# Seven products for eight in one more product of gate and up (S3 T3), with new orders of the stages

## The chip, the cores and the metric

The kernel runs on one core of one Trainium2 chip. The metric is the device time in microseconds (us), taken as the median of several runs.

## What is computed

Two layers in float32 on x of shape (2, 2048, 512). The first is an attention over the embedding axis: q, k, v are products of the normalized x with 512 x 512 weights, the scores are a 512 x 512 matrix for each of the two batches. The second is a gated network whose weights are looked up in a table of 16 values:

```
x = x + attention(layernorm(x))            # scores = q^T k / 4, softmax, times v, times Wo
n = layernorm(x)
gate = n @ lut[gate_idx].T                 # 1376 features
up   = n @ lut[up_idx].T
out  = x + (silu(gate) * up) @ lut[down_idx].T
```

The change lies in the two products with 1376 features, gate and up, which take 461 of 1063 us.

## The kernel before, in words

**Stages in time.** Gram matrices of the normalized x (to 80 us), 512 x 512 products for the scores and weights (to 174), the attention's output y (to 286), gate and up (286 to 747), the last 96 features by rows (747 to 789), the down product (to the end).

**Gate and up.** The 1376 features are 10 blocks of 128 (index f) and a rest of 96; the 4096 tokens are 8 chunks of 512, taken in 4 pairs (index p). A unit is one block and one pair (class `GateUp`, L1071). Gate and up of a block, and the two chunks of a pair, form a 2 x 2 scheme of blocks, whose 8 block products are made with 7 (Strassen's scheme in Winograd's form): "11"x"11" (stage a1), "S2"x"T2" (a2), "S1"x"T1" (a3), "S4"x"22" (a4), "S3"x"T3" (c1), "22"x"T4" (c2), "12"x"21" (b). Each is two matmuls of 128 x 128 by 512 columns, since a half of the 512 inputs is two blocks of 128. The results add up in PSUM (2 KB banks of 128 x 512) and, copied by ACT or added by DVE, in SBUF: p1, p7 (what c1 gives), u2, c22, h0, h1 and y. A hidden chunk h0 or h1 goes to DRAM (`hd`) by SP's queue.

**Second level.** From f = 2 on, four units form a group: two blocks (f even, f + 1) and two pairs (p even, p + 1). Within a group three of the seven products are themselves made with 7 matmuls for 8, by class `Second` (L948): `of_b` for "12"x"21", `of_c` for "22"x"T4", `of_d` for "S4"x"22", in the PSUM banks x, z and w. A unit's place in its group is its role: 0 (f even, p even), 1 (f even, p odd), 2 (f odd, p even), 3 (f odd, p odd). Roles 0 and 1 of a group follow each other; so do 2 and 3, but they come a whole row of units later (order of units: f, then p). So partial sums that roles 0 and 1 make for roles 2 and 3 are kept in DRAM: `part` (L1010) copies a bank with ACT and stores it as r6 or r5. Role 1 stores both for each `Second` on ACT's queue. Role 2 adds a further product onto r5 by an accumulating DMA from POOL (`onto=True`). They come back through `add_part` (L1023), an accumulating DMA from DRAM onto p1 or u2, or through `back` (L1028), a plain load into y, both from POOL: r6 in role 2, r5 in role 3. The second level's sums of tokens (T1, T2, T4 of each `Second` and group) are made once, kept in DRAM (`far`), and loaded by ACT's queue before each use (`loads`, L1049): for role 1 T1 and T2, for role 2 T4. Their buffers are rings: RT = 3 for parts, TT = 8 for these loads (L1034). p1, p7, c22, y and h1 have one buffer each, u2 and h0 two.

**Order.** PE, ACT, DVE and SP keep the order in which the program writes their instructions; POOL's is set by the framework's scheduler. `Line.run` (L1239) writes the stages of a unit, with those of the unit before mixed in: a4, first, end and out of the last unit stand within the present one. `between` (L1376) is called between stages: it issues a waiting T load, runs a waiting side job, and then fills DVE with lookups of later weights as long as a planned DVE clock is less than `leads[0]` us ahead of a planned PE clock. Lookups (`copy_predicated`, L342, and `tensor_scalar`, L330) are DVE's largest work.

**Banks.** PSUM has 8: a and c twice, b, x, z and w once (L945). The down product uses a, b and c as well.

**Last rows.** `LastRows` (L1294) computes the 96 last features with the tokens on the rows; every second pair needs sums and negatives of the weights (`weights`), written as side jobs.

Of the kernel before, what the change touches and what calls it, by code (L numbers as in the profile page):

```python
# [69 lines left out]
def tile_attn_ffn(  # L70
# [874 lines left out]
    def psum(tag, name):  # L945
        return fps.tile([P, E], F32, tag=tag, name=name, bufs=2 if tag in "ac" else 1)

    class Second:  # L948
# [8 lines left out]
        def sums(self, g):  # L957
# [4 lines left out]
            def made(tag, u, v):  # L962
                r[tag] = x2p.tile([P, CH], F32, tag="tt", name=f"{tag}_{self.name}{g}", bufs=TT)
                sub(r[tag], u(), v())
                far = self.far[g, tag] = dram.tile(
                    [P, CH], F32, tag=f"{self.name}{g}{tag}", name=f"far_{self.name}{g}{tag}"
                )
                nc.gpsimd.dma_start(far, r[tag])
# [12 lines left out]
        def ready(self, f):  # L981
            return f in gu if self is of_d else f in uw
# [45 lines left out]
        def back(self, u):  # L1028

            t = u.temp("y")  # L1030
            nc.gpsimd.dma_start(t, self.parts[u.p // 2, {2: "r6", 3: "r5"}[u.role]])
            return t

    RT, TT = 3, 8  # L1034
# [7 lines left out]
    seconds = [of_c, of_b, of_d]  # L1042
# [6 lines left out]
    def loads(f, p):  # L1049

        g = p // 2
        if 1 < f < NFT - 1 and f % 2 == 0 and p % 2:
            order = [(of_c, "T2"), (of_c, "T1")]
            order += [(o, tag) for tag in ("T2", "T1") for o in (of_d, of_b)]
        elif 1 < f < NFT - 1 and f % 2 and p % 2 == 0:
            order = [(o, "T4") for o in seconds]
        else:
            order = []
        return [lambda o=o, tag=tag: o.load(g, tag) for o, tag in order]
# [11 lines left out]
    class GateUp:  # L1071
# [32 lines left out]
        def extra0(self):  # L1104
            if self.role == 1:
                of_c.go_on(self, "S2", "T2")
                of_c.part(self, "r6")
            elif self.role == 2:
                of_c.begin(self, "S3", "T3")
                of_c.part(self, "r5", onto=True)  # L1110

        def c1(self):
            self.c = self.view("c")
            mm(self.c, self.pairs("S3", "T3"), True)
            self.p7 = self.temp("p7")
            evict(self.p7, self.c)
# [7 lines left out]
        def c2(self):  # L1124
            if self.role is None:
                mm(self.c, self.pairs("22", "T4"), False)
                add(self.u2, self.c, self.u2)
            elif self.role == 0:
# [3 lines left out]
                add(self.u2, self.c, self.u2)  # L1132
            elif self.role == 1:
                add(self.u2, self.c, self.u2)
                of_c.go_on(self, "S4", "22")
                add(self.u2, of_c.ps, self.u2)
            elif self.role == 2:
                of_c.go_on(self, "22", "T4")

        def extra1(self):  # L1140
            if self.role == 1:
                of_c.go_on(self, "S1", "T1")
                of_c.part(self, "r5")
            elif self.role == 2:
                of_b.begin(self, "S3", "T3")
                of_b.part(self, "r5", onto=True)

        def extra2(self):
            if self.role == 1:
                of_d.go_on(self, "S2", "T2")  # L1150
                of_d.part(self, "r6")
                of_b.go_on(self, "S2", "T2")
                of_b.part(self, "r6")

        def extra3(self):
            if self.role == 1:
                of_d.go_on(self, "S1", "T1")
                of_d.part(self, "r5")
                of_b.go_on(self, "S1", "T1")
                of_b.part(self, "r5")  # L1160
            elif self.role == 2:
                of_d.begin(self, "S3", "T3")
                of_d.part(self, "r5", onto=True)
            if self.role in (2, 3):
                self.y = of_d.back(self)

        def b(self):
# [14 lines left out]
            if self.role != 1:  # L1182
                nc.scalar.activation(h0, self.p1 if self.role in (None, 3) else h0, AF.Silu)

        def silu(self):

            if self.role == 1:
                nc.scalar.activation(self.h0, self.h0, AF.Silu)

        def a3(self):  # L1190
            mm(self.a, self.pairs("S1", "T1"), False)
            self.c22 = self.temp("c22")
            add(self.c22, self.a, self.p7)

        def first(self):
            if self.role == 2:
                add(self.u2, of_c.ps, self.u2)
            if self.role in (2, 3):
                add(self.u2, self.c, self.u2)
            tensor(self.h0, self.h0, self.u2, ALU.mult)  # L1200
            self.store(self.h0, 2 * self.p)

        def kept(self):
            add(self.y, of_d.ps, self.y)
# [28 lines left out]
    class Line:  # L1233
# [5 lines left out]
        def run(self, u, final=False):  # L1239
            last, self.last = self.last, u  # L1240

            role = getattr(u, "role", None)
            u.a1()
            if last is not None:
                last.silu()
            self.between()
            before = getattr(last, "role", None)
            if before == 1:
                last.first()
            u.extra0()  # L1250
            u.c1()
            self.between()
            if before == 2:
                last.kept()
            elif before == 3:
                last.first()
            u.extra1()
            if role != 3 and last is not None:
                last.a4()
                self.between()  # L1260
            u.a2()
            if role == 3:
                self.between(0.0)
                last.a4()
                last.first()
                self.between(0.0)
            else:
                self.between()
            u.extra2()
            u.c2()  # L1270
            if last is not None:
                last.end()
            self.between()
            u.extra3()
            if last is not None:
                last.out()
            one, two = (u.a3, u.b) if final or role in (1, 3) else (u.b, u.a3)
            one()
            self.between()
# [3 lines left out]
            self.between()  # L1283
# [10 lines left out]
    class LastRows:  # L1294
# [17 lines left out]
        def weights(self):  # L1312
            w, v = self.w, self.v
            self.u = u = last_pool.tile([P, KB, 2 * LAST], F32, tag="last", name="last_2")
# [7 lines left out]
                lambda: minus(u[:, 3, :], v[:, 0, :], -1.0),  # L1322
            ]

        def pairs(self, c):

            w, v, u, x = self.w, self.v, self.u, xs[c // 2]
            second = c // 2 % 2
            if c % 2 == 0:
                one, two = (("11", w[:, 0:2, :]), ("21", w[:, 2:4, :], u[:, 0, :], u[:, 1, :]))  # L1330
            else:
                one, two = (("T3", v[:, 2:4, :]), ("22", v[:, 0:2, :], u[:, 2, :], u[:, 3, :]))
            t = x[one[0]]
            out = [(t[:, kk, :], one[1][:, kk, :]) for kk in range(2)]
            t = x[two[0]]
            if second:
                return out + [(t[:, 1, :], two[2]), (t[:, 0, :], two[3])]
            return out + [(t[:, kk, :], two[1][:, kk, :]) for kk in range(2)]
# [35 lines left out]
    leads = [1.4]  # L1374
# [102 lines left out]
    class Down:  # L1477
# [36 lines left out]
        def view(self, tag):  # L1514
            return psum(tag, f"{tag}_d_{self.name}")[:, :H]
# [61 lines left out]
        extra0 = extra1 = extra2 = extra3 = silu = end = out = first  # L1577
# [34 lines left out]
    for (f, p), following in zip(units, units[1:] + [(NFT, 0)]):  # L1612
# [11 lines left out]
        to_load[:] = loads(*following)  # L1624
# [30 lines left out]
    todo += by_two(last_rows.weights() + down_sums(0, hps["dT"]))  # L1655
    n = 0
    for c in (0, 4, 2, 6, 1, 5, 3, 7):
        for half in range(2):
            ps = last_rows.products(c, half, n)
            if n == 0:  # L1660
                line.flush()
            last_rows.rows(c, half, ps)
# [103 lines left out]
```

## Time and profile before

| | us |
|---|---|
| runs | 1064.05, 1063.87, 1063.44 |
| median | 1063.87 |
| profiled execution, its time | 1064.37 |
| its span, first to last instruction | 1062.6 |
| busy: DVE, ACT, POOL | 803.3, 385.1, 108.6 |
| gate and up: start, end | 286.3, 747.1 |

The profile is one execution. Busy time is that of instructions; DMA issues and waits of an engine do not count as busy. A float32 matmul appears as two records, so 128 matmuls are x256. A DMA's share is the part of a stretch in which the 16 DMA engines worked on packets, as a mean over the 16; q0 is POOL's queue, q1 SP's, q10 ACT's. "us to landing" runs from the start of the issuing instruction to the event that says that the data is there. Granted clock was 1.00 throughout.

### The profile page before, as it was taken

Reading aid. Unit: us, or ns where it says so; the run is one execution under the profiler, and the core shown is the slowest. Engines: PE = TensorE matmul, PEld = TensorE weight load, DVE = VectorE, ACT = ScalarE, POOL = GpSimd, SP = SyncE. Lnnn points to the kernel's source line nnn. Section 1 sums busy time; section 2 is a strip of 40 time slices with the busy share of each in tenths; the row PEclk is TensorE's granted clock in tenths of the full one; section 3 lists DMA queues with packets and bytes.
Section 4 is the critical chain, followed back from the end, with each engine's and each line's share of the span. In section 5 each row is a group of like instructions: output and inputs, shape, how many; then the busy total and the mean of one; then the engine's idle time right before and its main releaser. Section 6 shows DMA issues by size and latency. Waiting matters only on the chain.

```text
span 1062.6 us, 11343 instructions
## 1 busy us (share of the span) xinstructions
PE 1055.5 (99%) x3554; PEld 661.3 (62%) x3554; DVE 803.3 (76%) x1538; ACT 385.1 (36%) x725; POOL 108.6 (10%) x160
## 2 busy tenths in 40 slices
PE   8999999999999999999999999999999999999998
PEld 5668887444444444444444444444998888888887
DVE  7888788898998897887988868849756455656554
ACT  4652532455542224444443444444222222211111
POOL 0000000012120120230141023014000000000000
PEclk9999999999999999999999999999999999999999
DMA  8650314589571366696697679569747665666773
GB/s 342 224 186 21 74 25 119 137 225 250 153 217 41 133 232 197 166 201 209 198 188 215 199 170 222 190 205 195 238 149 244 204 211 187 194 195 203 226 227 117
DMA packets 129084, 194.69 MB, mean 183 GB/s; under 512 B 18992, under 2 KB 59184, under 8 KB 127872
## 3 DMA queue, kind: packets, MB, share of 16 engines
q1 hardware_dynamic: 75904, 105.81, 31.4%
q0 software_dynamic: 15776, 39.92, 17.9%
q10 hardware_dynamic: 37344, 48.24, 14.0%
q8 instruction: 28, 0.46, 0.2%
q14 instruction: 32, 0.26, 0.1%
HBM read 111.42 MB, written 82.51 MB: 183 GB/s over the span
## 4 chain that ended last, share of the span: by engine, by line
PE 97%; DVE 1%; ACT 1%; DMA 0%; issue 0%; SPq 0%; ACTq 0%
PE a_g L1065 22%; PE a_d L1065 14%; PE y L839 10%; PE c_g L1065 8%; PE c_d L1065 7%; PE gp L522 6%; PE rows L1349 4%; PE b_d L1065 4%; PE x_g L1065 4%; PE z_g L1065 4%; PE w_g L1065 3%; PE b_g L1065 2%; PE ea_t L675 1%; PE ea_p L675 1%; PE ea_m L675 1%; PE ea_s L675 1%
## 5 line engine op out<-in xcount | busy, mean ns | idle before, releaser
L839 PE MATMUL y<-m,nT 128*128 128x512 f32 x256 | 110.2, 592 | 0.0
L342 DVE COPY_PREDICATED w<-b_w,w 128x1024 f32<-128x1024 int16 (+1 forms) x77 | 98.6, 1280 | 1.4
L839 PEld LDWEIGHTS y<-m,nT 128*128 128x128 f32 x256 | 48.5, 190 | 60.5 <-issue 57.3
L1065 PE MATMUL a_g<-xT_a,s 128*128 128x512 f32 x160 | 75.5, 594 | 0.0
L1065 PE MATMUL a_g<-xb,w 128*128 128x512 f32 x160 | 75.3, 593 | 0.0
L1065 PE MATMUL c_g<-xb,w 128*128 128x512 f32 x160 | 75.2, 592 | 0.0
L1065 PE MATMUL a_d<-dT,hs_a 128*128 128x256 f32 x288 | 72.6, 379 | 0.0
L522 PE MATMUL gp<-xn_a 128*128 128x128 f32 (+3 forms) x256 | 69.9, 434 | 1.7 <-DVE xn_a L223 1.7
L330 DVE TENSOR_SCALAR w<-idx_w,lut_x,lut_sb 128x1024 int32<-128x1024 int32 (+1 forms) x88 | 67.7, 794 | 0.2
L522 PEld LDWEIGHTS gp<-xn_a 128*128 128x128 f32 x256 | 43.9, 190 | 28.4 <-issue 15.1
L172 DVE TENSOR_TENSOR r<-r,p_d 128x256 f32<-128x256 f32 x64 | 27.1, 424 | 44.4 <-ACT p_d L181 41.5
L1065 PEld LDWEIGHTS a_d<-dT,hs_a 128*128 128x128 f32 x288 | 54.5, 189 | 7.7
L1065 PE MATMUL a_g<-xT_sq,s 128*128 128x512 f32 x120 | 56.7, 595 | 0.0
L181 ACT COPY p_d<-a_d 128x256 f32<-128x256 f32 x32 | 11.9, 372 | 121.4 <-PE a_d L1065 121.4
L1065 PEld LDWEIGHTS a_g<-xT_a,s 128*128 128x128 f32 x160 | 30.1, 190 | 38.9 <-issue 36.4
L1065 PEld LDWEIGHTS a_g<-xb,w 128*128 128x128 f32 x160 | 30.3, 190 | 38.5 <-issue 35.9
L1065 PEld LDWEIGHTS c_g<-xb,w 128*128 128x128 f32 x160 | 30.4, 190 | 38.3 <-issue 37.3
L342 DVE COPY_PREDICATED wd<-b_wd,wd 128x1024 f32<-128x1024 int16 (+1 forms) x42 | 50.7, 1208 | 0.8
L172 DVE TENSOR_TENSOR r<-r,a_d 128x256 f32<-128x256 f32 x64 | 26.8, 419 | 29.5 <-PE a_d L1065 29.5
L181 ACT COPY u<-a_g 128x512 f32<-128x512 f32 x40 | 23.4, 586 | 59.9 <-PE a_g L1065 57.3
L172 DVE TENSOR_TENSOR c<-a_g,p 128x512 f32<-128x512 f32 x40 | 27.6, 691 | 20.4 <-PE a_g L1065 19.0
L1349 PEld LDWEIGHTS rows<-last,xb 128*128 128x128 f32 x256 | 41.7, 190 | 0.5 <-issue 0.5
(357 smaller groups left out, 2086.2 us busy)
## 6 DMA issues: line engine op xcount, KB each, us to landing
hd<-h SPq DMA_DIRECT2D x80, 256.0 KB, 3.3
h<-hd SPq DMA_DIRECT2D x40, 512.0 KB, 6.3
nl<-nd SPq DMA_DIRECT2D x32, 256.0 KB, 5.8
xnd<-xn_f ACTq DMA_DIRECT2D x16, 512.0 KB, 4.6
fl<-xnd POOLq DMA_DIRECT2D x32, 256.0 KB, 6.1
xn_back<-xnd SPq DMA_DIRECT2D x32, 256.0 KB, 4.0
rd<-r SPq DMA_DIRECT2D x32, 256.0 KB, 3.2
r<-rd SPq DMA_DIRECT2D x32, 256.0 KB, 4.5
```

The costliest lines, as they stand in the source:

```text
L172: nc.vector.tensor_tensor(dest, a, b, op)
L181: nc.scalar.copy(dest, a)
L330: vec.tensor_scalar(dest.bitcast(I32), idx, lut_x[:rows, k : k + 1], lut_i[:rows, at : at + 1], ALU.bitwise_and, ALU.bitwise_xor,)
L342: vec.copy_predicated(dest, masks[level - 1], t)
L522: nc.tensor.matmul(gp[b][i][:, i * P :], xn[:, i, j % 2, :], xn[:, i:, j % 2, :], start=c % CPB == 0 and j == 0, stop=c % CPB == CPB - 1 a ...
L675: nc.tensor.matmul(ps[:, m, :], self.a[a][:, k, m * P : (m + 1) * P], self.b[b][:, k, :], start=first and m == k == 0, stop=k == 1, skip_g ...
L839: nc.tensor.matmul(ys[k], nTs[k][:, i, :], m[:, i, :], start=(i == 0), stop=(i == KB - 1))
L1065: nc.tensor.matmul(ps, lhsT, rhs, start=first and i == 0, stop=i == len(pairs) - 1, skip_group_check=not first,)
L1349: nc.tensor.matmul(ps[:, jj, :], x[:, j * P : (j + 1) * P], w, start=i == 0, stop=i == len(pairs) - 1,)
```

## The change

A fourth `Second`, `of_e`, makes the product "S3"x"T3" of the four units of a group with 7 matmuls of 128 features for 8, in a PSUM bank e; c then has one bank. What changes by role (in matmuls and in transfers of 256 KB):

- role 0: c1's two matmuls become one that begins e (copied by ACT to bank c) and one onto c.
- role 1: c1's two become three on e (S2 T2, S1 T1, S4 22); two parts more are copied by ACT and stored by its queue; four more T loads for each group and even block go to the ring, of which one is issued late, within role 1.
- role 2: c1's two become two on e (S3 T3, 22 T4); p7 is loaded from r6 of e by POOL, and a part more is added onto r5 by POOL. p7 is then added to u2 by DVE.
- role 3: c1's two go; p7 is loaded from r5 of e by POOL, and r5 of e is also added onto u2 by POOL, after r5 of c.

In the built program, of matmuls with 512 columns there are 691 for 699; ACT has 16 more copies and 40 more DMA issues, POOL 38 more DMA issues, DVE 8 more sums of 512 columns, 16 of 128 and one of 192. The first matmuls of blocks 4, 5 and 6 stand 61 and 45 matmuls apart before, 63 and 41 after.

POOL's order in block 5, by the built program (onto: a part added onto DRAM; r: role): p7 (r2), p1 (r2), onto c, onto e, onto b, u2 (r2), two idx loads, onto d; p7 (r3), p1 (r3), u2 from c (r3), y (r3), u2 from e (r3); p7, p1, onto c, y, onto e, onto b, u2, onto d (r2); p7, p1, u2 from c, y, u2 from e (r3). The y of the first role 2 comes earlier, in block 4.

The core of the diff:

```diff
-        return fps.tile([P, E], F32, tag=tag, name=name, bufs=2 if tag in "ac" else 1)
+        return fps.tile([P, E], F32, tag=tag, name=name, bufs=2 if tag == "a" else 1)
...
-                r[tag] = x2p.tile([P, CH], F32, tag="tt", name=f"{tag}_{self.name}{g}", bufs=TT)
+                r[tag] = x2p.tile([P, CH], F32, tag="rt", name=f"{tag}_{self.name}{g}", bufs=RT)
...
-    RT, TT = 3, 8
+    RT, TT = 3, 7
...
-    seconds = [of_c, of_b, of_d]
+    of_e = Second("e", "e", lambda f: in_two(gu[f]["S3"]), lambda p: in_two(xs[p]["T3"]))
+    seconds = [of_c, of_b, of_d, of_e]
...
+        def c0(self):
+            of_e.begin(self, "11", "11")
+            self.c = self.view("c")
+            evict(self.c, of_e.ps)
+
+        def kept(self, o, a, b, tag, onto=False):
+            (o.begin if onto else o.go_on)(self, a, b)
+            o.part(self, tag, onto)
...
+        def e4(self):
+            of_e.go_on(self, "S4", "22")
+            self.p7 = self.temp("p7")
+            evict(self.p7, of_e.ps)
+            add(self.u2, of_e.ps, self.u2)
+
+        def e3(self):
+            of_e.go_on(self, "22", "T4")
+            add(self.p7, of_e.ps, self.p7)
...
         def a3(self):
             mm(self.a, self.pairs("S1", "T1"), False)
             self.c22 = self.temp("c22")
             add(self.c22, self.a, self.p7)
+            if self.role == 2:
+                add(self.u2, self.p7, self.u2)
...
+            of_last("silu")
             u.a1()
+            if role == 3:
+                u.p7 = of_e.back(u, "p7")
+                last.c3()
+                last.y_kept()
+                go(0.0)
+                u.a2()
+                go(0.0)
+                of_last("a4", "first")
+                go(0.0)
+                u.y = of_d.back(u, "y")
+                of_e.add_part(u, u.u2)
+                last.end()
+                go()
+                last.out()
+                u.a3()
+                go()
+                u.b()
+                go()
+                return
...
+            if role == 1:
+                u.kept(of_c, "S2", "T2", "r6")
+                go()
+                u.kept(of_e, "S2", "T2", "r6")
+            elif role == 2:
+                u.p7 = of_e.back(u, "p7")
+                u.kept(of_c, "S3", "T3", "r5", True)
+                go()
+                u.kept(of_e, "S3", "T3", "r5", True)
+                u.kept(of_b, "S3", "T3", "r5", True)
+            else:
+                u.c1() if role is None else u.c0()
+                go()
+            if last is not None:
+                last.a4()
+                go()
+            if role == 1:
+                u.kept(of_c, "S1", "T1", "r5")
+            u.a2()
+            go()
+            if before == 3:
+                last.first()
+            if role == 1:
+                u.kept(of_e, "S1", "T1", "r5")
+                u.kept(of_d, "S2", "T2", "r6")
+                u.kept(of_b, "S2", "T2", "r6")
+                u.c4()
+            elif role == 2:
+                u.kept(of_d, "S3", "T3", "r5", True)
+                u.y = of_d.back(u, "y")
+                u.e3()
...
+            if role == 1:
+                u.e4()
+                u.kept(of_d, "S1", "T1", "r5")
+                u.kept(of_b, "S1", "T1", "r5")
...
-    leads = [1.4]
+    leads = [1.7]
...
-            return psum(tag, f"{tag}_d_{self.name}")[:, :H]
+            return psum("ce"[self.jj] if tag == "c" else tag, f"{tag}_d_{self.name}")[:, :H]
...
-        to_load[:] = loads(*following)
+        to_load[:] = loads(f, p, late=True) + loads(*following)
```

The Silu of h0 of a role 3 unit moves from that unit's stage b to the start of the next unit (`silu`), ahead of that unit's copy of p1 on ACT. `of_e` changes T3 of every second pair in place, as `of_b` and `of_d` do with their operands; so `LastRows` takes other weights for T3 there, with one sum of weights more. Its sums are written one step later, after the first row product. In the down product c takes the banks c and e by turns.

## The prediction

> **What bounds the kernel now.** The page comes first: the busy row of the engines, then the chain that ended last.
>
> ```profile
> PE 1055.5 (99%) x3554; PEld 661.3 (62%) x3554; DVE 803.3 (76%) x1538; ACT 385.1 (36%) x725; POOL 108.6 (10%) x160
> ...
> PE 97%; DVE 1%; ACT 1%; DMA 0%; issue 0%; SPq 0%; ACTq 0%
> ```
>
> PE works 1055.5 of 1062.6 us and is 97% of the chain. So a matmul that goes is worth its whole time, as long as nothing else takes PE's place. What could is read stage by stage, since shares over the whole span are averages. Gate and up runs from 286.3 to 747.1 us: 536 matmuls of 512 columns in 460.8 us, 0.859 us each, without a gap (the waits of PE in this window hold no entry). From feature block 2 on, even and odd blocks alternate. Here are block 4 and block 5, in the view by stretches (busy PE, PEld, DVE, ACT, POOL, then clock, DMA share, GB/s):
>
> ```profile
> 473.50:525.90 52.40, 52.40 (x123) 23.18 (x122) 44.01 (x62) 22.85 (x39) 2.09 (x4) 1.00 0.65 205
> 525.90:564.50 38.60, 38.60 (x91) 16.93 (x90) 34.15 (x57) 16.18 (x28) 15.48 (x18) 1.00 0.88 185
> ```
>
> The last but one column is the one to look at: in the odd block the DMA engines are busy 0.88 of the time, at fewer GB/s than in the even one. The DMA view of the odd block says with what:
>
> ```profile
> q0 software_dynamic: 2190, 4.46, 67.8%
> q1 hardware_dynamic: 890, 1.59, 11.3%
> q10 hardware_dynamic: 576, 1.05, 9.0%
> ```
>
> The shares of the three queues add up to the 0.88, so the queues use the same engines in turn. The even block has this:
>
> ```profile
> q10 hardware_dynamic: 3744, 6.82, 39.9%
> q1 hardware_dynamic: 1414, 2.60, 13.6%
> q0 software_dynamic: 464, 1.31, 11.6%
> ```
>
> From these rows comes the price of one transfer of 256 KB, as time of all 16 engines. q10: 20.9 us for 26 transfers, **0.80** each. q1: 7.1 us for 9.9, **0.72**. q0 (issued by POOL) mixes plain loads and adds: 6.1 us for 5 in the even block (1 add, 4 plain by its list of issues), 26.2 us for 17 in the odd one (13 adds, 4 plain). Solved: an **add 1.68**, a plain load on q0 **1.10**. An add costs over twice a plain transfer.
>
> Is this a limit, or only latency? In the odd block 3 POOL issues seven transfers from 438.02 to 445.73. The first lands 4.2 us after its issue, the last 7.4 us:
>
> ```profile
> p<-part_r_b POOLq DMA_DIRECT2D x1, 256.0 KB, 4.2
> ```
> ```profile
> part_r_d<-r_d POOLq DMA_DIRECT2D x1, 256.0 KB, 7.4
> ```
>
> Between the landings at 444.3 and 453.1 lie three adds, two plain loads, two stores of h and most of a load of T4: 5.0 + 2.2 + 1.4 + 0.6 = 9.2 us of work in 8.8 us. The queue builds up and is served at a rate of 1.0 to 1.05. After 457 it is empty again (the next add takes 4.0). So in the odd blocks DMA is just about full, and PE does not feel it yet.
>
> **The change part by part.**
>
> *Matmuls.* By the instruction lists PE loses 8 matmuls of 512 columns (699 to 691), one for each of 8 groups: 8 x 0.859 = **-6.9 us**. Between the first matmuls of its blocks, an even one goes from 61 to 63 (54.1 us), an odd one from 45 (38.6 us) to 41 (35.2 us).
>
> *DMA in the odd blocks.* Before, an odd block needs 14 adds (4 to p1, 4 to u2, 6 of parts onto DRAM), 6 plain loads on q0 (4 y, 2 idx), 8 stores of h, 3 loads of T4: 23.5 + 6.6 + 5.8 + 2.4 = 38.3 us, against 38.6 us of PE. After, `of_e` adds two parts onto DRAM, two second adds to u2 (role 3) and four loads of p7, and one T4: 18 adds, 10 plain, 8 stores, 4 T4: 30.2 + 11.0 + 5.8 + 3.2 = **50.2 us against 35.2 us**. Work is moved into the stretch that has no room, and PE's time there is cut.
>
> *What of this reaches PE.* Count from the first matmul of an odd block. The add to p1 of its last unit must land before ACT's Silu of h0, which now stands ahead of the next unit's copy of p1 on ACT; that unit's a2 waits for the copy. Up to and with that add lie 16 adds, 8 plain loads, about 7 stores and 4 T4: 43.9 us. The first data can move at about 2.6 us (p7's load waits for DVE's last use of the buffer, and is issued in 0.57). Landing comes 1.0 us after the last byte (in the burst the first add: bytes from 439.5, 1.68 of service, landed at 442.2). At a rate of 1.0 that is 47.5, at 1.06 (the bins of 2 us from 450 to 456 read 1.05 to 1.07) 45.0; Silu 0.63 and copy 0.57 follow, so a2 starts at 46.2 to 48.7. Undisturbed it starts 44 matmuls in, at 37.8. That is 8.4 to 10.9 us late.
>
> Two more waits lengthen it. POOL takes its issues in order: the second add to u2 waits until the first has landed, and p7's next load waits for DVE's u2 += p7, which waits for an add (p7 has one buffer). Behind them stand the adds to p1 and the parts. With the queue as long as above, each can leave it dry for 1 to 1.5 us, to 13 us in all. From the other side: with no queue at all, landings of 4.2 to 5.3 us as in the empty stretches, the chain in an odd block's third unit is: matmul 28, the end of a2, at 24.0; u2 copied at 24.9; its add issued behind three parts at 26.7, landed at 32; DVE 0.7; p7's and p1's issues (0.57 and 0.9), landed at 38.5; Silu and copy. That puts a2 at 39.9, 2 us late. ACT's fourth part also waits, for a buffer (RT is 3) whose add lands after 5.2 us; that is inside the same bound. So an odd block loses between 2 and 13 us; I take **9.5**, from the service times, because the burst shows them as a limit. Block 9 is counted the same, although the row products behind it give PE four banks, 32 products of 0.326, before it needs ACT. Four odd blocks: **+38 us**.
>
> One rule of the Trainium skill speaks against this: "DMA: Bandwidth & Descriptors", section "Anatomy of one DMA — SWDGE (gpsimd) path", gives a transfer about 2.0 us fixed and its bytes over 436 GB/s. By it 256 KB are 0.60 us of data, the 40 transfers of an odd block 24 us, and nothing would be late (1057 us). The page says nothing of adds; the rows above have 1.68 us for one, and the rows decide.
>
> *DVE.* 16 sums of 128 columns (0.28), 8 of 512 (0.69), one of 192 (0.35): 10.3 us more. DVE is idle some 76 us of gate and up, and the lookups that the planner fills in are moved by it; nothing, and 10.3 us if that cover were gone. The lead of 1.7 for 1.4 only moves lookups.
>
> *ACT.* 16 copies (0.59) and 40 issues (0.33). They fall mostly in role 1, where eight parts for six are copied and issued, 1.04 us apart against 0.86 for a matmul. The longest run, e, d and b one after another, leaves ACT some 0.3 us behind at p7's copy, and the matmuls that need the copied banks come 0.6 us or more after each copy. Nothing; at worst 1 us in each of 8 units. The even blocks' DMA grows by 9 transfers of 0.80, to some 37 of 54 us: covered.
>
> *PSUM, last rows.* One bank for c where there were two: in blocks 0 and 1 the next c1 comes six matmuls (5.2 us) after c2, whose sum takes 0.69. Down takes c and e by turns. The row weights' sums come one step later, before a product that is 10 us away. Nothing; 0.7 us for each of 8 units if the sum were late.
>
> **Sum**: span 1062.6 - 6.9 + 38 = 1093.7; the profiled execution took 1064.37, 1.8 more than its span, so 1095.5; the median of the runs is 0.5 below it: **1095**.
>
> **The rivals.**
>
> 1. *Hidden after all, faster.* The adds of one queue overlap with the other queues and with each other, so 50 us of service fit in 35 us. It decides if the engines take 1.4 times what they took. For it: single bins read 1.2 to 1.8, PE shows no wait at 0.88. Against: over whole bursts the rate is 1.0. Then 1064.4 - 6.9 - 0.5 = 1057. Chance 0.14.
> 2. *Only the chain of landings.* The queue keeps up, but each odd block still loses the 2 us of the empty chain, up to 5: 4 x 2 to 4 x 5 less 6.9, 1065 to 1077. It needs a rate of about 1.25. Chance 0.17.
> 3. *Worse.* POOL's waits and the queue add up in every unit, over 13 us an odd block, or ACT is late in role 1 as well: with 16 us, 4 x 16 - 6.9 gives 1121. For it: u2's sum now holds DVE in order. Against: what is late also gives DMA time to catch up. Over 1110: chance 0.06.
> 4. *The forecast*, 1078 to 1110, most likely 1095: 0.63.
>
> **How the numbers follow.** About 0.2% (2 us) is what a measurement of this kernel can tell from no change. Faster: rival 1 and a sliver of rival 2, 0.15. Within 0.2%: 0.05, from the low end of rival 2. Slower: 0.80. The range leaves out rival 1 and rival 3, and goes from 1062 to 1110.
>
> **What would show it.** Right: PE idle in the odd blocks alone, in front of a2 of units after role 3 and of a1, released by ACT's copy of p1 or by DVE; landings of POOL's adds growing from 4 to beyond 10 us within an odd block; a DMA share near 1.0 there; ACT waiting for the add to p1 in front of its Silu; odd blocks of 42 to 48 us, even ones of 54. Wrong: odd blocks of 35 us with the share below 0.9 (rival 1), landings that stay at 4 to 6 us while PE still waits (rival 2), or PE idle in the even blocks (ACT, PSUM or DVE, which I priced at nothing).

## The result and the profile after

| | before | after |
|---|---|---|
| median of the runs, us | 1063.91 | 1115.74 |
| ratio, 95% interval | | 1.0493 (1.0474 to 1.0511) |
| span of the profiled execution, us | 1062.6 | 1113.2 |
| PE busy, us | 1055.5 | 1067.6 |
| PE idle (span less busy), us | 7.1 | 45.6 |

The changed kernel is 51.8 us slower. The forecast said slower, at 1095; the time lies 6 us above the upper end of its range, 1110. The page of after has these lines (busy time; clock by slices; chain of what ended last):

```profile
PE 1067.6 (96%) x3538; PEld 660.4 (59%) x3538; DVE 811.2 (73%) x1563; ACT 390.4 (35%) x741; POOL 134.0 (12%) x198
...
PEclk9999999999999999989989998999899999999999
...
PE 73%; DMA 9%; issue 7%; DVE 5%; ACT 3%; POOL 2%; ACTq 0%; POOLq 0%; SPq 0%; DVEq 0%
```

The first line gives the account. The span grew by 50.6. PE's idle time grew by 45.6 - 7.1 = **38.5**. PE's busy time grew by 12.1, though 8 matmuls (6.9) are gone; so the other matmuls took **19.0** longer. The second line says why: the granted clock, 1.00 throughout before, falls below 0.9 in four of the 40 slices. 38.5 + 19.0 - 6.9 = 50.6.

By stretches (length, busy PE, PEld, DVE, ACT, POOL, then clock, DMA share, GB/s), the odd blocks 3, 5, 7, 9 and the even block 4:

```profile
448.50:488.50 40.00, 32.16 (x68) 13.18 (x67) 25.27 (x44) 11.81 (x21) 15.75 (x21) 0.87 0.95 212
488.50:549.00 60.50, 60.50 (x142) 26.30 (x141) 50.80 (x78) 28.48 (x50) 6.58 (x10) 1.00 0.72 232
549.00:588.00 39.00, 31.72 (x69) 13.16 (x68) 24.96 (x44) 11.60 (x20) 17.39 (x22) 0.91 0.96 219
...
648.00:689.00 41.00, 34.95 (x75) 14.53 (x74) 25.89 (x44) 13.04 (x23) 18.88 (x25) 0.92 0.94 208
...
749.00:790.00 41.00, 35.06 (x74) 14.49 (x73) 26.16 (x38) 13.67 (x25) 19.84 (x23) 0.92 0.95 213
```

PE is idle 7.8, 7.3, 6.1 and 5.9 us in the odd blocks, 27.1 together, and the clock is below 1.00 in the same stretches. The rest of the 38.5 lies in the even blocks' stretches (6.7, small waits) and in one wait of the row products behind block 9 (5.0). The waits of PE that are longest in sum (total, times, longest):

```profile
PE a_g L1065 <- ACT p L181: 26.1, 8, 7.7
PE rows L1379 <- DVE hrow L1392: 5.0, 1, 5.0
PE x_g L1065 <- ACT r_b L1014: 2.6, 4, 1.2
```

So PE mostly waits in front of a2 for ACT's copy of p1, as the forecast said: once in each odd block, in its last unit, for 7.7, 6.4, 5.1 and 5.1 us (24.3 of the 26.1). Followed back in block 3, the wait of 7.7 us looks like this. POOL, in the order of time (start, duration, then what it was idle for before):

```profile
458.07 0.69 POOL L299 DMA_DIRECT2D idx_w<-in_gate_idx_dram  x1
...
459.17 1.06 POOL L1026 DMA_DIRECT2D u<-part_r_c  x1
459.97 0.83 POOL L1030 DMA_DIRECT2D y<-part_r_d  x1
467.76 0.87 POOL L1026 DMA_DIRECT2D u<-part_r_e  x1 [6.96 <-DMA u<-part_r_c]
468.32 0.87 POOL L1030 DMA_DIRECT2D p<-part_r_e  x1
468.86 1.23 POOL L1026 DMA_DIRECT2D p<-part_r_b  x1
469.42 1.57 POOL L1016 DMA_DIRECT2D part_r_c<-r_c  x1
```

POOL stands still for 7 us: the second add to u2 (from e) waits for the first (from c) to land. Over the whole kernel such waits take 27.4 us, in 7 places. The next unit's p7, its p1 and the parts are queued behind it and go out within 4 us, in one burst. ACT then:

```profile
477.30 0.59 ACT L1014 COPY r_d<-w_g 128x512 f32<-128x512 f32 x1 [9.38 <-DMA part_r_c<-r_c]
477.78 0.63 ACT L1214 ACTIVATE h<-h 128x512 f32<-128x512 f32 x1
479.78 0.63 ACT L1173 ACTIVATE h<-h 128x512 f32<-128x512 f32 x1 [1.36 <-DVE h L172]
480.31 0.57 ACT L181 COPY p<-a_g 128x512 f32<-128x512 f32 x1
```

ACT's copy of the fourth part needs the buffer of the first, whose add was late by POOL's stand; 9.4 us are lost there, and the copy of p1 is three instructions further on. PE starts a2 at 480.93, and four of its records (two matmuls) take 3.78 us instead of 1.9:

```profile
480.93 3.78 PE L1065 MATMUL a_g<-xT_x,s 128*128 128x512 f32 x4 [7.71 <-ACT p L181]
```

The granted clock is 0.50 from 476.0 to 486.2 us, so PE runs the first 5.3 us after this pause at half speed.

### The profile page after: what moved, and what is told of

It reads as the page before. It is cut to its first block, busy times and chain, and to the rows that moved or that the text cites. A ratio compares the mean times of both kernels' runs of the same rounds, so it can differ in the third digit from the quotient of the medians.

```text
span 1113.2 us, 11497 instructions
## 1 busy us (share of the span) xinstructions
PE 1067.6 (96%) x3538; PEld 660.4 (59%) x3538; DVE 811.2 (73%) x1563; ACT 390.4 (35%) x741; POOL 134.0 (12%) x198
## 4 chain that ended last, share of the span: by engine, by line
PE 73%; DMA 9%; issue 7%; DVE 5%; ACT 3%; POOL 2%; ACTq 0%; POOLq 0%; SPq 0%; DVEq 0%
PE a_d L1065 14%; PE a_g L1065 12%; PE y L839 10%; PE c_d L1065 7%; PE gp L522 6%; PE b_d L1065 4%; DMA part_r_c<-r_c 3%; PE c_g L1065 3%; PE rows L1379 3%; PE x_g L1065 2%; PE e_g L1065 2%; PE z_g L1065 2%; DMA hd<-h 1%; PE w_g L1065 1%; PE b_g L1065 1%
## 5 line engine op out<-in xcount | busy, mean ns | idle before, releaser
L172 DVE TENSOR_TENSOR r<-r,p_d 128x256 f32<-128x256 f32 x64 | 27.1, 424 | 45.9 <-ACT p_d L181 40.0
L1065 PEld LDWEIGHTS a_g<-xT_a,s 128*128 128x128 f32 x160 | 29.2, 190 | 43.5 <-issue 31.6
L1065 PE MATMUL a_g<-xT_x,s 128*128 128x512 f32 x40 | 26.4, 795 | 24.2 <-ACT p L181 24.2
L1379 PE MATMUL rows<-last,xb 128*128 128x192 f32 x256 | 43.7, 335 | 5.0 <-DVE hrow L1392 5.0
L1065 PEld LDWEIGHTS a_g<-xT_sq,s 128*128 128x128 f32 x120 | 23.1, 194 | 31.3 <-issue 26.7
```

The source lines that it names most:

```text
L172: nc.vector.tensor_tensor(dest, a, b, op)
L1065: nc.tensor.matmul(ps, lhsT, rhs, start=first and i == 0, stop=i == len(pairs) - 1, skip_group_check=not first,)
L1379: nc.tensor.matmul(ps[:, jj, :], x[:, j * P : (j + 1) * P], w, start=i == 0, stop=i == len(pairs) - 1,)
```

## Experiments

Theories at the start: **service** (the forecast's: the DMA engines' time is used up, 50.2 us of work in 35.2 us), **POOL's order** (the second add holds the queue), **buffer** (RT is 3), and, for the 19 us of PE time, **clock** (a pause of PE halves the clock for a while). Ratios are against the kernel before, with 95% intervals. Labels are those of the quoted expectations.

### Is it the transfers of `of_e`, and which?

**e_none**: without `of_e`'s stores and adds. p7 is set to zero, so the outputs lack `of_e`'s part.

```diff
 def part(...):        nc.scalar.copy(t, self.ps)
+                      if self is of_e: return
 def back(...):
+                      if self is of_e: nc.gpsimd.memset(t, 0.0); return t
-                of_e.add_part(u, u.u2)
```

> The changed kernel without any of of_e's transfers through POOL and without its stores: its parts are copied by ACT and go nowhere, p7 is set to zero in roles 2 and 3, and the second add onto u2 is left out. Matmuls, stage orders, copies, sums and the loads of T stay. If the loss comes from transfers (theory: service of the DMA engines; rival: ACT waiting for a part's buffer; rival: POOL held by the second add onto u2), all three expect 1056 to 1062, with a granted clock of 1.00. If ACT's copies, the one bank of c or DVE cost PE anything, some of the 38 us of idle PE stay: 1070 or more.

Measured 1074.32, 1.0103 (1.0077 to 1.0128). So 41 us of the 52 come with these transfers. The three theories of transfers expected 1056 to 1062 and missed; the last branch, 1070 or more, came true. Some 17 us above the 1057 of the matmuls alone remain: PE is idle for 17.4 us against 7.1 before, and its matmuls take 5.8 us longer than their number explains. One wait of DVE in block 3 shows a kind that nobody had priced:

```profile
468.51 0.69 DVE L172 TENSOR_TENSOR h<-a_g,y 128x512 f32<-128x512 f32 x1 [5.93 <-DMA hd<-h]
```

h1 has one buffer. Its store had not landed when the next unit, two matmuls shorter than before, wrote it again. From 430 to 790 us DVE waits 18.5 us for h's stores, against 2.2 before. That this is what costs PE time is not shown: before_stores2, below, has 17.9 us of the same wait and loses only 4.7. The new order has a price of its own without `of_e`'s stores and adds; ACT's copies, POOL's writing of the zeros and the added loads of T are part of it here.

**dve_sum**: DVE adds p7 to u2 in role 3, as it does in role 2, instead of the second add.

```diff
-                of_e.add_part(u, u.u2)
-            if self.role == 2:
+            if self.role in (2, 3):
                 add(self.u2, self.p7, self.u2)
```

> Role 3 adds p7 to u2 with DVE, as role 2 does, in place of the second adding transfer from DRAM (two adds fewer in an odd block, and POOL has nothing that waits for the first add's landing). Service theory: 2 x 1.68 = 3.4 us less per odd block, so 4 x 3.4 = 14 us of stalls and some of the clock: 1095 to 1102. POOL theory: the 7 us that POOL stood still go, the rest of the block moves up by 5 to 7 us: 1070 to 1085. Buffer theory: the fourth part still waits for the first part's add, 5 to 6 us as in the first group, where PE did not feel it: 1075 to 1090.

Measured 1097.1, 1.0311 (1.0288 to 1.0335): 18.6 us less than after, the largest single part. It is less than POOL's order alone would give (1070 to 1085), and inside the range of the service theory (1095 to 1102).

**rt4_tt6** (after with `RT, TT = 4, 6`) and **dve_sum_rt4** (dve_sum with the same):

> Four buffers for parts (RT 4) and six for T (TT 6, for room): the fourth part of a role 2 unit no longer waits for the first one's add. Buffer theory: ACT's 9.4 us in front of the copy of r_d goes, and with it most of the 7.7 us that PE stands: 1070 to 1085. Service and POOL theories: the next thing in line, p7 and the add to p1, is as late as before, PE stands later in the block or in front of the next: 1095 to 1112.

> Both edits: sum by DVE in role 3, and four buffers for parts, six for T. Service theory: 46.8 us of service against 35 us of PE in an odd block, so some 5 us late in each, and the clock with it: 1078 to 1092. Buffer and POOL theories together: both waits are gone, 1058 to 1068.

Measured 1118.47, 1.0509 (1.0491 to 1.0527), and 1091.14, 1.0258 (1.0243 to 1.0273). The first is 2.7 us above after, and above every expectation: the wait for the part's buffer, ACT's longest in the trace of after, is worth nothing by itself. With it gone the waits move: PE's waits for ACT's p1 fall from 26.1 to 15.8 us, and 10.1 us behind DVE's h and 10.7 at the row products (5.0 before) take their place. Only with the second add gone as well does the buffer bring 6 us. 1091 again lies in the range of the service theory (1078 to 1092), not in that of the two waits together (1058 to 1068). So far the service theory has met two of its three expectations; the next runs test its price directly.

### Is the engines' time the limit?

**before_stores2**: the kernel before, with 16 more stores of 256 KB in each odd block, by SP, to scratch memory. By the forecast's prices that is 38.3 + 11.5 = 49.8 us of service in 38.6 us, where after has 50.2 in 35.2. The added ones are plain stores, on SP's queue. **before_stores2_even** puts them into the even blocks.

```diff
         def store(self, h, c):
+            if self.role in (2, 3):          # (0, 1) in before_stores2_even
+                for _ in range(2):
+                    nc.sync.dma_start(scratch[k], xs[self.p]["11"][:, 0, :])
```

> The kernel before, with two stores of 256 KB more after each store of h in roles 2 and 3 (16 in an odd block), from a tile of tokens that nobody overwrites to DRAM that nobody reads: nothing computed waits for them. That is 16 x 0.72 = 11.5 us of DMA service more in each odd block, about as much as the change adds (11.9), with no wait, no POOL instruction and no buffer of the change. Service theory: 49.8 us of service in 38.6 us: odd blocks 6 to 10 us longer, with the slower clock after it 1090 to 1112. Wait theories (POOL held, parts' buffers, p7's chain): landings grow by a few us, PE feels little of it: 1064 to 1072.

> The same 16 stores per block, in the even blocks instead: 34 + 11.5 = 46 us of service in 52.4 us. Service theory: fits, 1063 to 1068. If 64 more stores cost by themselves (SP's issue, HBM), they cost the same here as in the odd blocks.

Measured 1068.48, 1.0052 (1.0032 to 1.0073), and 1063.86, 1.0001 (0.9991 to 1.0010). The first is 4.7 us, in the range of the wait theories (1064 to 1072) and far from that of service (1090 to 1112). Service as a fixed price falls. Block 5 of before_stores2, by stretches and by queues:

```profile
525.90:564.50 38.60, 38.60 (x91) 16.93 (x90) 33.26 (x55) 15.96 (x27) 15.43 (x18) 1.00 0.96 245
```
```profile
q0 software_dynamic: 2063, 4.23, 58.9%
q1 hardware_dynamic: 2282, 4.14, 29.2%
```

PE has no gap. q1 moves 4.14 MB instead of 1.59 in the same 38.6 us, and the core 245 GB/s instead of 185. q1's price per byte is the old one (0.292 x 38.6 = 11.3 us, 2.7 us per MB, as before); q0's fell from 26.2 us for 4.46 MB to 22.7 for 4.23. A share of 0.88 was no wall. The adds did land later, in the median 5.9 us for 4.8 (p1) and 5.1 for 4.6 (u2's first), and PE hardly felt it.

The trace of before also shows why the prices misled. In block 5 more than 16 packets are in flight at once in 43% of the time, and up to 25, on 16 engines. The times of packets overlap, so their sum over 16 is not the time that the engines need.

**before_pool2**: the same 16 stores issued by POOL, to load q0 itself.

> The kernel before, with the same 16 extra stores per odd block as in before_stores2, issued by POOL in place of SP: same bytes, other queue. Theory that the adds' queue q0 is served one transfer after the other, and that transfers of the other queues fit in between: q0 goes from 26 us to 26 + 16 x 1.10 = 44 us in 38.6 us; the adds that stages wait for come late behind them, 5 us or more per odd block and a slower clock after it: 1085 to 1105. Theory that all queues share one service time: as before_stores2, 1066 to 1072. POOL's own time (16 issues of 0.57 to 0.97 us beside 15.4) fits in both.

Measured 1063.83, 1.0000 (0.9991 to 1.0010), but the test didn't test: POOL's order is the scheduler's, and it put all 64 stores between 259 and 375 us, ahead of the odd blocks from 3 on. What more work on POOL's queue does to them stays open, and with it the narrower theory that the adds of q0 alone are slow to serve one another.

**dve_sum_hw** and **dve_sum_rt4_hw**: dve_sum, with three or four buffers for parts, and the plain loads of p7, y and the indices issued by SP instead of POOL.

> The same with RT 3 and TT 7: the fourth part waits for the first one's add again. With q0 no longer overfull that add should land in 5 to 6 us, as in the first groups of before, and cost PE nothing: within 4 us of dve_sum_rt4_hw. If the buffer matters by itself: 8 to 20 us slower than it.

> The changed kernel with the sum by DVE in role 3, RT 4 and TT 6, and with all plain loads taken from POOL's queue: p7, y and the index loads are issued by SP. q0 keeps 16 adds in an odd block, 26.9 us of 35.2 (0.76, against 0.68 before). Queue theory: almost no stalls, 1057 to 1066. One service time for all queues: 43 us in 35.2, as dve_sum_rt4 or 3 us per block better: 1078 to 1088. If SP's order (a load that waits holds the stores of h behind it) takes the place of the waits, DVE waits for h's buffers: 1070 to 1085.

Measured 1096.03, 1.0306 (1.0290 to 1.0323), against dve_sum's 1097.1, and 1094.41, 1.0286 (1.0256 to 1.0316), against 1091.14. Fewer plain loads in POOL's line buy nothing, where the theory of a full queue q0 expected 1057 to 1066. The test is not clean, since other waits take the place of those that shrink: in dve_sum_hw, from 430 to 790 us, DVE waits 22.8 us for u2's adds, for 39.1 in dve_sum, but 10.0 for the loads of p7, which now land in 5.5 us for 3.0. Of u2's adds themselves the median landing stays long, 7.7 us for 7.3.

**before_short**: the kernel before, with PE's time in the odd blocks cut to that of after.

```diff
-            mm(self.c, self.pairs("S3", "T3"), True)
+            mm(self.c, self.pairs("S3", "T3")[: 1 if self.role in (2, 3) else 2], True)
```

> The kernel before, with one of the two matmuls of 128 features left out in c1 of roles 2 and 3 (that half of p7 is missing in the sums of these blocks, on purpose of nothing but PE's time): 16 matmuls less, 41 for 45 in an odd block as in the changed kernel, with the order of stages, the transfers and the buffers of before. If the odd block of before has room (only the added transfers cost): 16 x 0.859 = 13.7 less, 1050 to 1052. If its adds' landings already fill it, so that any cut of PE comes back as waits: 1056 to 1064. The fixed price of service (38.3 against 35.2 us) says 1062 to 1063.

Measured 1051.71, 0.9889 (0.9873 to 0.9906): 12.2 of the 13.7 us. PE waits nowhere in gate and up but once, 0.3 us. So the odd block of before had room for four matmuls less, and (before_stores2) for 16 transfers more. Neither the shorter block nor the added load alone makes the loss. Both together, and added load on POOL's queue, were not run. The reading that is left is that it matters *which* transfers are waited for, and how soon; the next runs look for them.

### Which wait holds the odd block?

In the traces of dve_sum and its kin, one chain repeats. The add to u2 lands late; DVE, which in the new a3 adds p7 to u2 in the same unit, stands in line for it; only then is p7's one buffer free for the next load, and on POOL the scheduler put the next add to p1 behind that load. The median landing of u2's first add over the whole kernel, before and after:

```profile
u<-part_r_c POOLq DMA_DIRECT2D x16, 256.0 KB, 4.6
```
```profile
u<-part_r_c POOLq DMA_DIRECT2D x16, 256.0 KB, 7.0
```

**two_p7** (after) and **dve_two_p7** (dve_sum), both with two buffers of p7, `RT, TT = 3, 6`:

> The changed kernel with two buffers of p7 for one (and six of T for seven, which makes the room); nothing else. Its POOL then need not wait, with a load of p7, for DVE's u2 += p7 of the unit before, but still waits, with the second add to u2, for the first one's landing (7 us in block 3). If the one buffer of p7 is the main cause, 1070 to 1090. If POOL's wait for the first add alone is what counts, the loads of p7 only change their place in its line: 1105 to 1120. If the service of the transfers sets the time, 1112 to 1120.

> DVE adds p7 to u2 in role 3 (as in dve_sum, 1097) and p7 has two buffers (T six). Theory, a chain through one buffer: the add to u2 lands, DVE adds p7, only then is the next p7 loaded, and p1's add stands behind that load on POOL, or DVE behind the load; both are gone here: 1062 to 1078. Rival, the landings as such (each unit's add to p1 must land before its Silu and the next copy, whatever stands before it): 1088 to 1098. Rival, seven or six buffers of T: a loss of some us.

Measured 1123.14, 1.0559 (1.0542 to 1.0576), and 1097.6, 1.0326 (1.0304 to 1.0349). The buffer alone buys nothing; with the second add kept the run is 7 us slower than after and above every expectation (it also has one buffer of T less). The second lies in the range of the rival, the landings as such (1088 to 1098). The chain through p7's buffer, taken by itself, falls.

**dve_late_two_p7**: that, with role 2's sum moved too, from a3 to the stage `first` (in the next unit, where the kernel before took its own last sum of u2), and `RT, TT = 4, 5`.

```diff
 def a3:    add(self.c22, self.a, self.p7)
-           if self.role in (2, 3): add(self.u2, self.p7, self.u2)
 def first:
+           if self.role in (2, 3): add(self.u2, self.p7, self.u2)
```

> As dve_two_p7, but role 2's u2 += p7 too stands late, ahead of the product with h0, where the kernel before has its own sum, and the parts have four buffers and T five. DVE then does not stand in line behind an add's landing ahead of h0's sums. Chain theory: 1057 to 1070, the best of all; landings as such: 1084 to 1095, as dve_sum_rt4 (1091); T's loads late with five buffers: PE waits for T in the even blocks, some us.

Measured **1083.13**, 1.0188 (1.0171 to 1.0205): 8 us below dve_sum_rt4, the best with all products, 13 us above the range of the chain theory and 1 below that of the landings. In its trace DVE waits for u2's adds 3.5 us from 430 to 790 us, where it waited 45.4 in dve_sum_rt4; what is left of PE's waits is nearly all in front of a2 for ACT's p1, 14.4 us in 8 waits.

**dve_rt4_two_p1**: dve_sum_rt4 with two buffers of p1, and the Silu of h0 behind the next copy of p1 on ACT.

```diff
-            of_last("silu")
             u.a1()
+            of_last("silu")
```

> dve_sum_rt4 (1091: DVE adds p7 to u2 in role 3, the parts have four buffers) with two buffers of p1 for one, T five, and the Silu of role 3's h0 (role 1's too) behind the next unit's copy of p1 on ACT, not ahead of it. The copy, and with it PE's a2, then no longer waits for the add to p1 of the unit before. If that add is what ends PE's waits: 1062 to 1078. If the adds to u2 with p7's load behind them, and the line on DVE, hold it: 1083 to 1092, PE's waits moving from ACT's copy to DVE or to the parts' copies.

Measured 1088.86, 1.0235 (1.0211 to 1.0258); its interval overlaps that of dve_sum_rt4, and it lies in the second range. PE's waits there summed to 11.3 us for DVE's h and 7.7 for ACT's p1; here:

```profile
PE a_g L1065 <- DVE h L172: 11.2, 9, 2.3
PE a_g L1065 <- ACT p L181: 10.5, 4, 4.2
```

and what holds DVE in block 3 is again u2's add, in front of the sum of h1 that frees PE's bank a:

```profile
465.29 0.69 DVE L172 TENSOR_TENSOR u<-p,u 128x512 f32<-128x512 f32 x1 [5.72 <-DMA u<-part_r_c]
...
468.44 0.68 DVE L172 TENSOR_TENSOR h<-a_g,y 128x512 f32<-128x512 f32 x1
```

**none_two_p7**: e_none with the late sum in roles 2 and 3 and two buffers of p7.

> As e_none (of_e's stores and adds left out, p7 set to zero by POOL, no second add to u2: the outputs lack of_e's part), with DVE's u2 += p7 late in roles 2 and 3, and two buffers of p7. What was left in e_none (1074, 17 above the 1057 of the matmuls alone) is then without the wait of p7's buffer for u2's add. Chain theory: 1056 to 1062. If the new order of the stages itself costs (matmuls fewer between a unit's copies and the next one's need, h1's one buffer, y's): 1068 to 1075.

The ratio is 1.0084 (1.0062 to 1.0106), some 1073 us, no different from e_none by the intervals: the second branch. What the new order costs without `of_e`'s stores and adds does not come from the early sum or p7's buffer. h1's one buffer is the candidate that e_none's trace shows; two buffers of h1 were not tried.

### The clock

**before_hold8** and **before_hold18**: the kernel before, where ACT repeats its copy of p1 8 or 18 times in the last unit of each odd block, so that PE pauses four times and nothing else changes.

```diff
-            evict(self.p1, self.a)
+            for _ in range(9 if self.role == 3 and self.p == NPR - 1 else 1):   # 19
+                nc.scalar.copy(self.p1, self.a)
```

> The kernel before, in which ACT copies p1 nine times for once in the last unit of each odd block: 8 x 0.53 to 0.59 = 4.2 to 4.7 us of ACT in front of a2, of which PE's slack takes 1.2 to 1.7. PE should stand about 3 us in each of four places. Theory that a pause costs only its length: 1063.9 + 12 = 1076. Theory that the granted clock falls after a pause (in the changed kernel it was 0.5 for some 5 us after the 7.7 us one): 1076 plus up to 4 x 3 = 1088, if 3 us are enough for it.

> As before, with 18 copies more: 9.5 to 10.6 us of ACT, PE standing about 8.5 us in four places. Pause alone: 1063.9 + 34 = 1098. With a granted clock of 0.5 for 5 to 7 us after each: 10 to 14 us more, 1108 to 1112, and a mean clock of 0.985 to 0.99.

Measured 1089.3, 1.0242 (1.0227 to 1.0257), and 1113.97, 1.0472 (1.0457 to 1.0488). Both times are near the theory of a slower clock (1088, and 1108 to 1112) and far from that of the pause alone (1076 and 1098). The pauses are 3.9 and 10.1 us. PE's busy time rises by 10.8 us in *both*, 2.7 for each pause on average, though one pause is 2.6 times as long as the other. PE works 17.9 and 19.0 us of this time at a clock of 0.50, which explains 9.0 and 9.5 of the 10.8. In before_hold18 PE stops at 468.9 and goes on at 479.0:

```profile
470.00:474.00 4.00, 0.00 (x0) 0.00 (x0) 0.36 (x1) 3.81 (x7) 0.00 (x0) 1.00 0.03 6
474.00:478.00 4.00, 0.00 (x0) 0.00 (x0) 0.00 (x0) 3.78 (x8) 0.00 (x0) 0.50 0.00 0
478.00:482.00 4.00, 3.00 (x4) 1.45 (x5) 0.00 (x0) 1.41 (x3) 0.87 (x1) 0.50 0.29 34
482.00:486.00 4.00, 4.00 (x8) 1.50 (x8) 1.51 (x3) 1.41 (x3) 1.42 (x2) 0.72 0.34 50
486.00:490.00 4.00, 4.00 (x11) 1.85 (x10) 3.76 (x6) 1.25 (x3) 0.01 (x1) 1.00 0.86 220
```

The clock (last but two) is 1.00 for the first 5 us of the pause, 0.50 from there until 484.2, 5.2 us after PE has resumed.

**before_hold_steps**: 3, 4, 5 and 6 extra copies in blocks 3, 5, 7 and 9, to find the shortest pause that costs.

> The kernel before, with 3, 4, 5 and 6 copies of p1 more in the last unit of blocks 3, 5, 7 and 9 (8 gave a pause of 3.9 us): pauses of about 1.2, 1.7, 2.2 and 2.8 us. Tells from which pause on the granted clock falls to 0.5, which cost 2.7 us in each place both after 3.9 and after 10 us. If any pause costs the clock: 1063.9 + 8 + 4 x 2.7 = 1083. If it needs more than 3 us: 1072.

Measured 1074.91, 1.0103 (1.0082 to 1.0125), between the two. The four pauses:

```profile
469.67 1.98 PE L1065 MATMUL a_g<-xT_x,s 128*128 128x512 f32 x4 [0.81 <-ACT p L1103]
```
```profile
562.52 1.98 PE L1065 MATMUL a_g<-xT_x,s 128*128 128x512 f32 x4 [1.43 <-ACT p L1103]
```
```profile
656.10 2.71 PE L1065 MATMUL a_g<-xT_x,s 128*128 128x512 f32 x4 [2.05 <-ACT p L1103]
```
```profile
751.79 2.83 PE L1065 MATMUL a_g<-xT_x,s 128*128 128x512 f32 x4 [2.67 <-ACT p L1103]
```

After 0.81 and 1.43 us the next matmuls run at full speed (1.98), after 2.05 and 2.67 they don't (2.71, 2.83). Around the third pause the stretches read:

```profile
654.10:657.20 3.10, 1.10 (x3) 0.63 (x4) 1.50 (x6) 2.34 (x5) 0.86 (x1) 1.00 0.73 199
657.20:660.60 3.40, 3.40 (x6) 1.33 (x5) 0.05 (x1) 0.59 (x1) 0.89 (x2) 0.50 0.54 77
660.60:664.00 3.40, 3.40 (x9) 1.47 (x9) 3.22 (x5) 1.15 (x2) 0.57 (x1) 1.00 0.73 117
```

The clock falls 1.1 us after PE has resumed, and stays at 0.50 for 3.4 us. The clock theory stands, but these four pauses don't give a shortest length that costs. In the other traces of this case pauses of 1.93, 1.94 and 2.02 us (dve_sum) were followed by a clock of 0.50, and pauses of 2.44 (dve_late_two_p7), 3.17 (dve_sum) and 3.29 us (rt4_tt6) were not. First a line of dve_late_two_p7, then one of dve_sum:

```profile
473.18 1.98 PE L1065 MATMUL a_g<-xT_x,s 128*128 128x512 f32 x4 [2.44 <-ACT p L181]
```
```profile
574.47 2.85 PE L1065 MATMUL a_g<-xT_x,s 128*128 128x512 f32 x4 [1.93 <-ACT p L181]
```

None below 1.9 us was, and all above 3.3 us were.

## Why the prediction was wrong

**The step that failed** is the one that read "I take 9.5, from the service times, because the burst shows them as a limit". Prices of engine time were taken from packets' busy shares, added, and set against PE's time; but the packets of block 5 overlap, up to 25 on 16 engines. before_stores2 added as much service to the same block and lost 4.7 us, where that theory expected 26 or more; before_short took PE's four matmuls away and gained 12.2 of 13.7. The sum for before, 38.3 us against 38.6, was not a block at its limit either: block 5's own row has 0.88 of 38.6, 34.0 us, since two of y's four loads, for one, are issued in the even block's stretch. What the runs showed in its place are waits for particular landings, through POOL's and DVE's order: 18.6 us go with the second add to u2, 6 more with a fourth buffer for the parts, 8 more when p7's sum also stands late and has a second buffer. The forecast knew the first of these, "the second add to u2 waits until the first has landed", and priced it at 1 to 1.5 us of a dry queue; in block 3 POOL stood for 7.0. Why u2's first add lands in 7.0 us for 4.6 is not shown.

**The term that was missing**, and that took the time out of the range, is PE's clock. No step asked what a pause does to the matmuls behind it. After has five pauses of about 5 us and more (four for ACT's p1, one at the row products), and in the five stretches of a 0.50 clock that follow PE works for 24.2 us, so it loses half of that, 12.1 us, 1.7 to 3.1 for each. This is 12.1 of the 19.0 us of longer matmuls; the other 6.9 are not accounted for. Without the 19.0 the sum of the other terms, 38.5 - 6.9, would have come out at 1064.4 + 31.6 = 1096, the forecast's number. That is luck in part: the 38.5 are the sum forecast, but not in its places and not by its mechanism.

**Point by point.**

- Matmuls, -6.9: not tested alone; before_short gave 12.2 us for 16 matmuls, where 13.7 would be the whole price.
- DMA, +38 of PE's idle time: 38.5 measured, but the agreement is of sums. 27.1 of it lies in the odd blocks (6.8 each, for 9.5 forecast), the rest where nothing was forecast.
- ACT "nothing; at worst 1 us in each of 8 units": 6.7 us idle in the even blocks, within the worst case; 1.6 of it is behind DVE, not ACT.
- The parts' buffer "is inside the same bound": right, in that four buffers alone brought nothing (1118.5).
- Block 9 "counted the same": its odd part was (5.9), but the row products lost 5.0 more.
- DVE at nothing: its busy time was covered, but its order was not. In dve_sum and its kin DVE stands for u2's add, up to 4.7 us at a time in dve_sum and 6.4 in dve_two_p7, with PE behind it.
- Rival 1 (hidden, 1057), and the rule of the Trainium skill that went with it: not seen. (That page does speak of accumulating transfers, but gives no time for them.) Rival 2 (only landings, 1065 to 1077): its mechanism is closest to what the runs show, its price of 2 to 5 us an odd block is not; it took landings of 4.2 to 5.3 us, and u2's first add lands in 7.0. Rival 3 (worse, POOL's waits, 1121) had the time nearly right, with a chance of 0.06, but not its sum: it took 16 us an odd block, where PE is idle for 6.8.
- What would show it: PE idle in front of a2, landings up to 10 us and a share of 0.95 were all seen, and yet don't show service; the same signs go with a chain of waits. A share near 1 with *adds* in it can't tell the two apart, a further transfer can.

**What stays open**: the 16 to 17 us that remain without `of_e`'s transfers (e_none, none_two_p7), and the 9 to 10 us between those and dve_late_two_p7; what more load on POOL's own queue does (before_pool2 did not put it there); and why two buffers of p7 make after slower (1123). No version here that computes the whole result beats the kernel before.

## What to carry to other kernels

Before engine shares are read as a limit, ask which landing is waited for, and how many matmuls lie between its issue and its first use; a change that uses an accumulated result in the same unit, or puts one add behind another on an in-order issuer, can pay the landing in full, with everything queued behind it: here 7.0 us in one place, and 18.6 us less without the second add. Add to each stall of PE what the clock takes behind it, and count stalls, not only their sum. Where one wait is removed and the time stays, look for the next one on the same chain before the theory is dropped: here a removal alone brought between -7 and 19 us, and three steps together 33.

## What the hardware showed that was not expected

- After a pause of PE the granted clock was 0.50 in stretches of 3.41 us or a whole multiple of it (3.41 to 13.65), in the traces of all the runs shown with a pause of PE. A stretch began up to 5.3 us after PE stopped, sometimes when it had already resumed, and cost PE 1.4 to 3.1 us (half of the time that it worked in it). Pauses between 1.93 and 3.29 us were followed by one in some places and not in others. The Trainium skill ("TensorE: Matmul & The Clock Gate", section "Part 1: The HAM clock gate") says that the clock falls to 4/8 after at least one idle window of about 3.4 us and comes back after about 3.4 us of sustained work. The 0.50 agrees, and so does the step of 3.41 us. By the page an estimate of the loss in one window is half of 3.4, 1.7 us; in before_hold_steps, where each of the two stretches is 3.41 us long and PE works all through, the clock gives the same. A pause of 1.93 us, shorter than a window, was enough, and PE worked at 0.50 for up to 6.2 us, longer than a window.
- 16 stores of 256 KB more in 38.6 us, with the DMA share already at 0.88, cost 4.7 us over four blocks: in block 5 GB/s went from 185 to 245, the share only to 0.96, and PE had no gap.
